# An attention and density kernel: bank-wise dependences for one-bank jobs, the last two density units in turn, and a later end for the density

## The chip, the cores and the metric

The kernel runs on one core of a Trainium2 chip. The metric is the device time of one execution in microseconds. The runs shown of the kernel before are 4967.25, 4970.23 and 4970.26 us, median 4970.23. A profile is one more execution, recorded by the hardware profiler.

In the text PE or TensorE is the matmul engine (PEld its weight loads), DVE or VectorE the vector engine, ACT or ScalarE the scalar engine, POOL or GpSimd the general engine, SP or SyncE the engine that issues most transfers.

## The reference, cut to what matters

The input is x, 8 images of 192 channels by 64 x 64 positions, all float32. Two layers follow one another, each with a residual addition.

```python
# layer 0: attention over the N = 4096 positions of an image, queries and keys of 24 channels
v = _gn(x)                                   # group norm, 32 groups
q = prelu(conv1x1(v, w1, b1), a1)            # [24, N]
k = prelu(conv1x1(v, w2, b2), a2)            # [24, N]
w = prelu(conv1x1(v, wa, ba), aa)            # [192, N]
score = softmax(q.T @ k, axis=2)
x = x + (score @ w.T).T
# layer 1: a density of every element, by a small network per channel (1-3-3-3-1)
y = _gn(x)
lower, upper = net(y - 0.5), net(y + 0.5)    # net: softplus(m) @ z + b, then z + tanh(f) * tanh(z)
s = -sign(lower + upper)
x = x + maximum(abs(sigmoid(s * upper) - sigmoid(s * lower)), 1e-6)
```

The group norm needs sums over a whole image, so the density of an image can start only when the attention of that image has ended; the queries, keys and values of an image need only the norm of the input.

## The kernel before, in words

The program is one long stream of attention steps, with all other work written between them by a planner that runs when the program is built. There is no loop on the chip: the order on each engine is the order in which the planner emits.

**The stream.** An image has 8 tiles of 512 queries (`NB`), and a tile has 16 steps (`STEPS`), each for 256 keys; so an image takes 128 steps (`IMG`) and the eight images 1024 (`last`). Step t does: the score products of step t+1 (`scores`, L738) into the PSUM tile `sc`; the products for the row maxima of a later tile (`max_step`, L669), 22 steps ahead (`LEAD`), into the PSUM tile `mx`, followed by their reduction on DVE (L677); the exponential on ACT (L742) from `sc` into `e`; and the products of `e` with the values (`attend`, L753). There is only one `mx` and one `sc` tile, each of two banks, so the products of a step wait until the reduction and the exponential of the step before have read them.

**Turns and jobs.** Two more PSUM tiles, `turns` (names `b0` and `b1`), of two banks each, take the attention sums of the tiles alternately. While one collects, the other serves as room for all other PSUM work: this is a *job*. `start_job` takes one job a step from a list ordered by rank, finds a room with enough free banks (`homes`, a tile and for each bank the step until which it is taken), hands the job a two-bank tile or one bank of it, and books its later parts with `at(step, function, costs)`. Jobs of one bank are:

- `norm_end`: the sums over a group by a product with `gavg` (mean L420, variance L433) and their readers on DVE (`second` L425, `third` L438), followed by `root` on ACT and `fourth` on DVE;
- `weights`: small products with the norm (L506, L511, L516), read by `offsets` on DVE (L525, L530);
- `keys`: the products for the keys (L573), read twice by ACT in `prelu` (L558), which DVE then combines (L561);
- `max_end`: the maxima of a tile are collected on DVE (L697, L700), transposed on PE (`turn`, L705) and added into the queries on DVE (`add`, L710).

Jobs of two banks are `queries` (L602), `values` (L630) and `finish` (the transposes L786 of a tile's outputs, and the residual addition L795 on DVE).

The dependences between instructions come from the tile framework. It knows a tile as a whole here: a write into one bank of `b0` waits for an earlier reader of the other bank of `b0` too.

**The head.** Before the stream the first image's queries, keys, values and the first maxima are made. There `homes` has four rooms at first: the two turns and two tiles `sc_head` and `mx_head` (`others`), which later carry the first maxima.

**The density.** An image's density is 12 units (`Unit`): two halves c, three channel thirds g, and s for lower and upper. A unit has 23 operations on DVE (`stt`, L995, all 128 x 1024) and its tanh and scaling operations on ACT (L963, L972, L978, L988). Up to three units are open at once (`units`, the oldest first). `density_step` runs at the end of each step: it gives each engine a credit and lets the open units emit while the credit is positive. For DVE the credit grows by `rate`, which is the time of the operations left of the oldest image divided by the steps left until step 10 of the image after next, and is capped at twice `rate`; other DVE work that the planner emits is taken from the credit. An operation on DVE that needs an ACT result needs it from an earlier step. When a pair s = 0, 1 of a third is done, `ending` forms the difference (POOL in the stream, DVE in the tail: `alone`, L1139 to L1149) and stores the result (L1161 and the transfers after it).

Units of image b are made when the second norm of image b is known, some 12 steps into the next image's attention. The density of the last image comes after the stream; there 11 of its 12 units do a part of their sums on PE (`product`, L936), in the PSUM tiles `b0`, `b1`, `sc_tail`, `mx_tail`. What is left of image 6 at step 1024 is emitted in the tail as well, in credits of `RATE` = 4.15 us a step.

**Loads.** The residual input `xc` of half an image has three buffers; a load is requested at steps 6 and 70 of an image and starts when a buffer is free, which is when the store of an earlier density's third g = 2 has been emitted. `finish` of a tile waits, in planner steps, until its half is loaded.

Of the kernel before, what the change touches and what calls it, by code (L numbers as in the profile page):

```python
# [17 lines left out]
def kernel(  # L18
# [306 lines left out]


    homes = []

    scratch = []
    for k, cols in (("a", F), ("b", 2 * C)):  # L330
# [3 lines left out]
            pair.append(u)  # L334
        scratch.append(pair)
    ready = [0, 0]

    def start_job(t):
        p = t % STEPS
        for n, (rank, make, hold, banks, cols) in enumerate(jobs):  # L340
            if stream[0] and (p < 3 or p + max(hold, 1) >= STEPS):
                continue
            rooms = [(pm, g) for pm, g in homes if sum(k <= t for k in g) >= banks]
            if not rooms:
                if rank < 2:
                    return
                continue
            k = [i for i in (1, 0) if ready[i] <= t and scratch[i][0].shape[1] >= cols]
            if cols and not k:
                continue  # L350
            del jobs[n]
            pm, guest = min(rooms, key=lambda r: max(r[1]))
            at_ = [i for i in range(2) if guest[i] <= t]
            for i in at_[:banks]:
                guest[i] = t + hold + 1
            if cols:
                ready[k[0]] = t + 2
            parts = make(pm if banks == 2 else pm[:, at_[0], :], scratch[k[0]] if cols else None)
            for i, fn, cost, act, pe in parts:
                at(t + i, fn, cost, act, pe)  # L360
            return
# [47 lines left out]
    def norm_end(key, n, t, then=None):  # L409
# [7 lines left out]

        def mean():
            pm = cell["pm"]
            nc.tensor.matmul(pm[:, 0:2], lhsT=gavg, rhs=cell["mv"], start=True, stop=True)  # L420

        def second():
            mv, pm = cell["mv"], cell["pm"]
            res = cell["res"] = small.tile([128, 2], F32, tag="nrm", bufs=4, name=f"nrm_{nm}")
            nc.vector.tensor_copy(res, pm[:, 0:2])  # L425
            dv = cell["dv"] = small.tile([128, 2], F32, tag="dv", name=f"dv_{nm}")
            nc.vector.tensor_tensor(dv[:, 0:1], mv[:, 0:1], res[:, 0:1], ALU.subtract)
            nc.vector.tensor_tensor(dv[:, 0:1], dv[:, 0:1], dv[:, 0:1], ALU.mult)
            nc.vector.tensor_copy(dv[:, 1:2], dv[:, 0:1])

        def variance():
            pm = cell["pm"]
            nc.tensor.matmul(pm[:, 2:4], lhsT=gavg, rhs=cell["dv"], start=True, stop=True)  # L433

        def third():
            res, pm = cell["res"], cell["pm"]
            ve = cell["ve"] = small.tile([128, 1], F32, tag="ve", name=f"ve_{nm}")
            nc.vector.tensor_tensor(ve, res[:, 1:2], pm[:, 2:3], ALU.add)  # L438
# [36 lines left out]

        def make(pm, _):
            cell["pm"] = pm
            return [
                (0, mean, 0.0, 0.0, 0.4), (1, second, 0.8, 0.0, 0.0),
                (2, variance, 0.0, 0.0, 0.4), (3, third, 0.4, 0.0, 0.0),  # L480
            ]
# [7 lines left out]
    def weights(b, then):  # L489
        res = norms[b, 0]  # L490
        cell = {}

        def scale():
            for k, src, n in (("q", w1r, 2), ("k", w2r, 1), ("v", wa_sb, 1)):
                d = wf[k, b] = fold.tile(
                    [128, 3, src.shape[2]], F32, tag=f"w{k}", bufs=n, name=f"w{k}_{b}"
                )
                nc.scalar.activation(d, src, AF.Copy, scale=res[:, 1:2])
            mb = cell["mb"] = fold.tile([128, 128], F32, tag="mb", name=f"mb_{b}")
            nc.vector.tensor_copy(mb, res[:, 0:1].to_broadcast([128, 128]))  # L500

        def products():
            pf = cell["pf"]
            p = slice(0, R)
            for g in range(3):
                nc.tensor.matmul(  # L506
                    pf[:, 0:2], lhsT=wf["q", b][p, g, :], rhs=res[p, 0:2],
                    start=g == 0, stop=g == 2,
                )
            for g in range(3):  # L510
                nc.tensor.matmul(  # L511
                    pf[:, 2:4], lhsT=wf["k", b][:, g, :], rhs=res[:, 0:2],
                    start=g == 0, stop=g == 2,
                )
            for g in range(3):
                nc.tensor.matmul(  # L516
                    pf[:, 4 : 4 + C], lhsT=cell["mb"][p], rhs=wf["v", b][p, g, :],
                    start=g == 0, stop=g == 2,
                )

        def offsets():
            pf = cell["pf"]
            for k, src, at_, n in (("bq", bq, 0, 2), ("bk", bk, 2, 1)):
                d = wf[k, b] = fold.tile([128, 2], F32, tag=k, bufs=n, name=f"{k}_{b}")
                nc.vector.tensor_tensor(  # L525
                    d[:, 0:1], src[:, 0:1], pf[:, at_ : at_ + 1], ALU.subtract
                )
                nc.vector.tensor_scalar(d[:, 1:2], d[:, 0:1], -1.0, None, ALU.mult)
            d = wf["ba", b] = fold.tile([128, C], F32, tag="ba", name=f"ba_{b}")
            nc.vector.tensor_tensor(d, ba_row, pf[:, 4 : 4 + C], ALU.subtract)  # L530
            then()

        at(now[0] + 1, scale, 0.3, 2.0)
        def make(pf, _):
            cell["pf"] = pf
            return [(0, products, 0.0, 0.0, 2.0), (1, offsets, 1.0, 0.0, 0.0)]

        at(now[0] + 3, lambda: job(make, 1))


# [8 lines left out]

    made = set()  # L550

    def prelu(name, dst, src, bias, nslope, u):


        def first():
            for i, sign in enumerate((1.0, -1.0)):
                b_ = bias[:, i : i + 1] if bias is not None else 0.0
                nc.scalar.activation(u[i], src, AF.Relu, bias=b_, scale=sign)  # L558

        def last():  # L560
            nc.vector.scalar_tensor_tensor(dst, u[1], nslope, u[0], ALU.mult, ALU.add)  # L561
            made.add(name)

        return first, last

    def keys(b, d, what, done):
        t = xi[what, b, d]

        def make(pk, u):
            if b not in kt:  # L570
                kt[b] = kpool.tile([128, N // 4], F32, tag="k", name=f"k_{b}")
            for g in range(3):
                nc.tensor.matmul(  # L573
                    pk[:, 0:P], lhsT=wf["k", b][:, g, :], rhs=t[:, g, :],
                    start=g == 0, stop=g == 2,
                )
# [4 lines left out]
            first, last = prelu(  # L581
                ("k", b, d), kt[b][p, at_ : at_ + P], pk[p, 0:P], wf["bk", b][p], nslope[p, 1:2],
                [x[p, 0:P] for x in u],
            )
            return [
                (0, lambda: None, 0.0, 0.0, 1.3), (1, first, 0.0, 0.9, 0.0),
# [104 lines left out]
    def max_end(b, n):  # L691
# [10 lines left out]
        def turn():  # L702
            pt = cell["pt"]
            for t in range(4):
                nc.tensor.transpose(pt[:, t * 128 : (t + 1) * 128], nm[:, t, :], ident)  # L705

        def add():
            u = (n % 2) * 256
            q = qt[b, n // 2][:, :, u : u + 256]
            nc.vector.tensor_tensor(  # L710
                q, q, cell["pt"].rearrange("p (s t) -> p s t", s=2), ALU.add
            )
            made.add(("max", b, n))

        def make(pt, _):
            cell["pt"] = pt
            return [(0, turn, 0.0, 0.0, 0.8), (1, add, 0.7, 0.0, 0.0)]

        at(now[0], collect, 0.4)
# [140 lines left out]
    class Unit:  # L860
# [146 lines left out]
        def more(self, k):  # L1007
# [6 lines left out]
            if (n, j) == (3, 2):  # L1014
                for q in range(3):
                    self.give(("l", 2, q))
                b, c, g, s = self.key
                if s == 1:
                    ending(b, c, g)

        def need(self):
# [244 lines left out]
    for d in range(NP):  # L1266
# [1 line left out]
            norm_stat((0, 0), 2 * d + k, flat(xi["first", 0, d], k))  # L1268
    spread()
    negatives()  # L1270
    others = [
        ps_sc.tile([128, 2, F], F32, tag="sc", name="sc_head"),
        ps_mx.tile([128, 2, F], F32, tag="mx", name="mx_head"),
    ]
    homes.extend((t, [0, 0]) for t in turns + others)

    def go_on():
# [103 lines left out]
```

## Time and profile before

| what | value |
|---|---|
| runs | 4967.25, 4970.23, 4970.26 us, median 4970.23 |
| the profiled execution's own time | 4970.59 us |
| its span, first to last instruction | 4968.6 us |
| granted TensorE clock, mean | 0.984 |
| busy in the span | PE 4785.8, DVE 4301.2, ACT 3202.4, POOL 513.9 us |
| first exponential of the stream | at 95.3 us |
| last exponential of the stream | at 4613.0 us |
| images 0 to 7 of the stream | 554.3, 569.9, 575.3, 572.8, 574.2, 572.8, 574.3, 524.1 us |
| after the stream | some 356 us |

The image times are read from the starts of the exponentials (L742): image b begins with the exponential of its step 0. The page sums busy time over the whole span; since the stages have different limits (the stream, the norm of the last image, its density), it is read together with tables of stretches. In lists of waits a line gives the waiting engine and instruction, what ended the wait, the total in us, the number of waits and the longest. A timeline's line gives start, duration, engine, line, operation, tiles and shapes, the number of instructions merged, and in brackets the idle time of the engine before it with what ended it.

### The profile page before, as it was taken

What the parts mean: (1) busy time and instruction counts of PE and PEld (TensorE: products, weight loads), DVE (VectorE), ACT (ScalarE), POOL (GpSimd) and SP (SyncE); (2) the same over time, 40 slices, a digit from 0 to 9 for tenths busy, and PEclk for the clock granted to TensorE, in tenths of its full rate; (3) what the DMA queues carried; (4) which work ended last, traced back from release to release, by engine and by line L of the source; (5) the groups of instructions that cost most, each with busy time, mean ns of one, the idle gap of its engine ahead of it and who ended that gap; (6) DMA issues with size and microseconds to landing.
All of it is one profiled execution on the core that took longest, in us unless ns stands there. A gap on an engine that the chain in (4) does not pass through costs nothing.

```text
span 4968.6 us, 69863 instructions
## 1 busy us (share of the span) xinstructions
PE 4785.8 (96%) x29152; PEld 3525.8 (71%) x29152; DVE 4301.2 (87%) x4442; ACT 3202.4 (64%) x3709; POOL 513.9 (10%) x506
## 2 busy tenths in 40 slices
PE   7999999999999999999999999999999999999596
PEld 5777777777777777777777777777777777777242
DVE  5433359999899989999899999999899999999888
ACT  2333346776667767777667766776677766776665
POOL 0000001111012110112011210110101110110000
PEclk9999999999999999999999999999999999999798
DMA  2000020011200111010200111011111111000000
GB/s 57 24 23 17 14 52 15 21 24 35 49 18 18 41 37 34 22 34 24 60 15 21 41 27 40 18 35 31 31 34 28 27 29 24 11 20 7 9 11 15
DMA packets 111953, 135.48 MB, mean 27 GB/s; under 512 B 14739, under 2 KB 93077, under 8 KB 111637
## 3 DMA queue, kind: packets, MB, share of 16 engines
q1 hardware_dynamic: 110432, 130.65, 10.9%
q8 instruction: 228, 3.74, 0.3%
q14 instruction: 89, 0.72, 0.1%
q10 hardware_dynamic: 1204, 0.37, 0.0%
HBM read 105.82 MB, written 25.17 MB: 26 GB/s over the span
## 4 chain that ended last, share of the span: by engine, by line
PE 73%; DVE 22%; ACT 3%; issue 1%; POOL 1%; DMA 0%; POOLq 0%; ACTq 0%; SPq 0%; DVEq 0%
PE b L753 43%; PE sc L738 17%; DVE d L995 14%; DVE rm L677 5%; PE b L630 3%; PE b L936 2%; PE b L602 1%; PE b L573 1%; PE mx L669 1%; PE sc_tail L936 1%; PE mx_tail L936 1%; PE b L786 1%; ACT d L988 1%; ACT d L963 1%; PE b L705 1%
## 5 line engine op out<-in xcount | busy, mean ns | idle before, releaser
L753 PEld LDWEIGHTS b<-v,e 128*128 128x128 f32 x16384 | 2668.4, 191 | 781.5 <-issue 781.5
L753 PE MATMUL b<-v,e 128*128 128x193 f32 x16384 | 2972.7, 335 | 0.0
L742 ACT ACTIVATE e<-sc 128x1024 f32<-128x1024 f32 x1024 | 1046.3, 1022 | 1422.6 <-PE mx L669 1373.3
L677 DVE TENSOR_REDUCE rm<-mx 128x1 f32<-128x1024 f32 x1002 | 1222.0, 1220 | 522.2 <-PE mx L669 518.5
L738 PE MATMUL sc<-q,k 25*128 25x512 f32 x4096 | 1159.7, 642 | 5.5 <-ACT e L742 5.2
L669 PE MATMUL mx<-k,q 24*128 24x512 f32 x4008 | 1135.6, 643 | 13.1 <-DVE rm L677 13.0
L995 DVE SCALAR_TENSOR_TENSOR d<-d,wsp,d 128x1024 f32<-128x1024 f32 x768 | 985.8, 1284 | 47.5 <-ACT d L988 35.4
L995 DVE SCALAR_TENSOR_TENSOR d<-d,lc,d 128x1024 f32<-128x1024 f32 x765 | 968.4, 1279 | 16.3 <-ACT d L972 3.3
L995 DVE SCALAR_TENSOR_TENSOR d<-d,tf,d 128x1024 f32<-128x1024 f32 x543 | 681.5, 1280 | 4.0 <-ACT d L978 3.9
L978 ACT ACTIVATE d<-d 128x1024 f32<-128x1024 f32 x543 | 570.1, 1055 | 70.8 <-DVE d L995 69.3
L738 PEld LDWEIGHTS sc<-q,k 25*128 25x128 f32 x4096 | 306.8, 183 | 238.6 <-issue 198.8
L1077 POOL MEMSET pause<- 128x1 f32 x240 | 23.7, 99 | 4007.4 <-DVE d L995 4007.4
L988 ACT ACTIVATE d<-d,cb,wsp 128x1024 f32<-128x1024 f32 x351 | 433.1, 1235 | 6.6 <-DVE d L995 5.3
L963 ACT ACTIVATE d<-xc,bn,wn 128x1024 f32<-128x1024 f32 x288 | 353.2, 1233 | 7.8 <-DVE bn L467 7.0
L669 PEld LDWEIGHTS mx<-k,q 24*128 24x128 f32 x4008 | 300.2, 183 | 40.1 <-DVE rm L677 39.9
L972 ACT ACTIVATE d<-xc,bn,wn 128x1024 f32<-128x1024 f32 x255 | 314.6, 1234 | 0.1
L1124 POOL TENSOR_TENSOR d<-d,d 128x512 f32<-128x512 f32 x80 | 167.9, 2098 | 0.1
L1112 POOL TENSOR_TENSOR d<-d,d 128x512 f32<-128x512 f32 x80 | 166.3, 2079 | 7.7 <-DVE d L995 7.1
L1132 POOL TENSOR_TENSOR d<-d,d 128x512 f32<-128x512 f32 x80 | 159.3, 1992 | 2.1 <-POOL pause L1077 0.3
L630 PE MATMUL b<-wv,xi 64*128 64x192 f32 x1344 | 139.5, 340 | 0.0
L630 PEld LDWEIGHTS b<-wv,xi 64*128 64x128 f32 x1344 | 106.5, 186 | 25.4 <-issue 23.8
L1116 ACT ACTIVATE d<-d 128x512 f32<-128x512 f32 x160 | 91.8, 623 | 32.1 <-POOL d L1112 26.0
(171 smaller groups left out, 2372.3 us busy)
## 6 DMA issues: line engine op xcount, KB each, us to landing
xi<-in_x_dram SPq DMA_DIRECT2D x392, 192.0 KB, 3.6
xc<-in_x_dram SPq DMA_DIRECT2D x64, 384.0 KB, 8.2
out_dram<-xc SPq DMA_DIRECT2D x96, 256.0 KB, 3.2
d<-in_x_dram SPq DMA_DIRECT2D x16, 192.0 KB, 4.3
d<-in_wat_dram ACTq DMA_DIRECT2D x2, 144.0 KB
cb<-in_den_b_dram SPq DMA_DIRECT2D x6, 2.2 KB, 2.1
ff<-in_den_f_dram SPq DMA_DIRECT2D x6, 2.2 KB, 2.1
bq<-in_b_dram ACTq DMA_DIRECT2D x4, 0.1 KB
```

Source lines behind the costliest of these rows:

```text
L630: nc.tensor.matmul(pv[:, s, 0:C], lhsT=t[p, g, k * 128 : k * 128 + 128] if g < 3 else one_row[p], rhs=wf["v", b][p, g, :] if g < 3 else wf ...
L669: nc.tensor.matmul(sc[:, s, :], lhsT=tile_of(qt[b, n // 2], n, j)[r], rhs=kt[b][r, u : u + F], start=True, stop=True,)
L677: nc.vector.tensor_reduce(out=rowmax[b, n][:, j, k : k + 1], in_=sc, axis=AX.XY, op=ALU.max)
L738: nc.tensor.matmul(sc[:, s, :], lhsT=kt[b][r, k : k + 128], rhs=qt[b, n // 2][r, :, u : u + 256], start=True, stop=True,)
L742: return lambda: nc.scalar.activation(e, sc, AF.Exp)
L753: nc.tensor.matmul(a[:, j, 0 : C + 1], lhsT=e[:, s, j * 128 : j * 128 + 128], rhs=v[:, s, p % 4, :], start=p == 0 and s == 0 and j % 2 == ...
L936: nc.tensor.matmul(out[:, h, :], lhsT=diag[g][:, 3 * i + n - 1 if n else 9 + i, :], rhs=src[:, h * F : h * F + F], start=n == 0, stop=n == 3,)
L963: nc.scalar.activation(self.buf[k], self.src(), AF.Tanh, bias=bn[:, s, g, 0, i : i + 1], scale=wn[:, g, 0, i : i + 1],)
L972: nc.scalar.activation(self.buf[k], self.src(), AF.Identity, bias=bn[:, s, g, 1, i : i + 1], scale=wn[:, g, 1, i : i + 1],)
L978: nc.scalar.activation(self.buf[k], self.buf["l", k[1], k[2]], AF.Tanh)
L988: nc.scalar.activation(self.buf[k], self.buf["l", n - 1, 0], AF.Identity, bias=offset, scale=wsp[:, g, w : w + 1],)
L995: nc.vector.scalar_tensor_tensor(dst, src, factor, dst, ALU.mult, ALU.add)
```

## The change

Three things are changed, and the order of the planner's decisions follows from them.

1. For one-bank jobs a matmul that writes bank i of a turn (or head tile) n is declared free of dependences on readers in the group `turn{n}{1-i}`, and each reader of bank i joins the group `turn{n}{i}`. It is done for `norm_end`, `weights`, `keys` and `max_end`; two-bank jobs are left as they were. The two head tiles are allocated earlier in the program, so that they have numbers.
2. When exactly two units are open, the one with more DVE operations left goes first, on each engine and in each step, and a unit is removed from the list when it has no DVE operation left, wherever it stands. The ending of a pair starts when both of its units are done, whichever is last.
3. `rate` counts the steps until step 15, not 10, of the image after next.

```diff
+    spot = [None]
+    def spotted():
+        n, i = spot[0]
+        def write(inst):
+            tc.declare_no_dep(inst.ins, group=f"turn{n}{1 - i}", reason="reads the other bank")
+        def read(inst):
+            tc.add_to_no_dep_group(f"turn{n}{i}", inst.ins)
+        return write, read
...
             if cols:
                 ready[k[0]] = t + 2
+            spot[0] = next(n for n, k in enumerate(turns + others) if k is pm), at_[0]
...
-            nc.tensor.matmul(pm[:, 2:4], lhsT=gavg, rhs=cell["dv"], start=True, stop=True)
+            cell["write"](
+                nc.tensor.matmul(pm[:, 2:4], lhsT=gavg, rhs=cell["dv"], start=True, stop=True)
+            )
...
-            nc.vector.tensor_tensor(ve, res[:, 1:2], pm[:, 2:3], ALU.add)
+            cell["read"](nc.vector.tensor_tensor(ve, res[:, 1:2], pm[:, 2:3], ALU.add))
...
+            write, read = spotted()
             for g in range(3):
-                nc.tensor.matmul(
+                write(nc.tensor.matmul(
                     pk[:, 0:P], lhsT=wf["k", b][:, g, :], rhs=t[:, g, :],
                     start=g == 0, stop=g == 2,
-                )
+                ))
...
                 b, c, g, s = self.key
-                if s == 1:
+                if not any(u.key == (b, c, g, 1 - s) and u.todo["DVE"] for u in units):
                     ending(b, c, g)
...
-            rate = left * COST["DVE"] / max(1, (units[0].key[0] + 2) * IMG + 10 - t) + OTHER
+            rate = left * COST["DVE"] / max(1, (units[0].key[0] + 2) * IMG + 15 - t) + OTHER
...
-            for n in range(min(3, len(units))):
+            order = list(range(min(3, len(units))))
+            if len(units) == 2:
+                order.sort(key=lambda n: -len(units[n].todo["DVE"]))
+            for n in order:
                 units[n].step(eng, t, list(units)[:n])
-        while units and not units[0].todo["DVE"]:
-            units.popleft()
+        for u in [u for u in units if not u.todo["DVE"]]:
+            units.remove(u)
```

The same wrapping by `write` and `read` is made in `weights` (`products`, `offsets`), in `max_end` (`turn`, `add`), in `norm_end`'s other two places and around the two ACT readers of the keys in `prelu`.

More of the change, by code (lines that the diff above doesn't have):

```diff
@@ L327 @@
     homes = []
+    others = [
+        ps_sc.tile([128, 2, F], F32, tag="sc", name="sc_head"),
+        ps_mx.tile([128, 2, F], F32, tag="mx", name="mx_head"),
+    ]
     scratch = []
@@ L419, in mean @@
             pm = cell["pm"]
-            nc.tensor.matmul(pm[:, 0:2], lhsT=gavg, rhs=cell["mv"], start=True, stop=True)
+            cell["write"](
+                nc.tensor.matmul(pm[:, 0:2], lhsT=gavg, rhs=cell["mv"], start=True, stop=True)
+            )
         def second():
@@ L424, in second @@
             res = cell["res"] = small.tile([128, 2], F32, tag="nrm", bufs=4, name=f"nrm_{nm}")
-            nc.vector.tensor_copy(res, pm[:, 0:2])
+            cell["read"](nc.vector.tensor_copy(res, pm[:, 0:2]))
             dv = cell["dv"] = small.tile([128, 2], F32, tag="dv", name=f"dv_{nm}")
@@ L432, in variance @@
             pm = cell["pm"]
-            nc.tensor.matmul(pm[:, 2:4], lhsT=gavg, rhs=cell["dv"], start=True, stop=True)
+            cell["write"](
+                nc.tensor.matmul(pm[:, 2:4], lhsT=gavg, rhs=cell["dv"], start=True, stop=True)
+            )
         def third():
@@ L477, in make @@
             cell["pm"] = pm
+            cell["write"], cell["read"] = spotted()
             return [
@@ L505, in products @@
             for g in range(3):
-                nc.tensor.matmul(
+                cell["write"](nc.tensor.matmul(
                     pf[:, 0:2], lhsT=wf["q", b][p, g, :], rhs=res[p, 0:2],
                     start=g == 0, stop=g == 2,
-                )
+                ))
             for g in range(3):
-                nc.tensor.matmul(
+                cell["write"](nc.tensor.matmul(
                     pf[:, 2:4], lhsT=wf["k", b][:, g, :], rhs=res[:, 0:2],
                     start=g == 0, stop=g == 2,
-                )
+                ))
             for g in range(3):
-                nc.tensor.matmul(
+                cell["write"](nc.tensor.matmul(
                     pf[:, 4 : 4 + C], lhsT=cell["mb"][p], rhs=wf["v", b][p, g, :],
                     start=g == 0, stop=g == 2,
-                )
+                ))
         def offsets():
@@ L524, in offsets @@
                 d = wf[k, b] = fold.tile([128, 2], F32, tag=k, bufs=n, name=f"{k}_{b}")
-                nc.vector.tensor_tensor(
+                cell["read"](nc.vector.tensor_tensor(
                     d[:, 0:1], src[:, 0:1], pf[:, at_ : at_ + 1], ALU.subtract
-                )
+                ))
                 nc.vector.tensor_scalar(d[:, 1:2], d[:, 0:1], -1.0, None, ALU.mult)
             d = wf["ba", b] = fold.tile([128, C], F32, tag="ba", name=f"ba_{b}")
-            nc.vector.tensor_tensor(d, ba_row, pf[:, 4 : 4 + C], ALU.subtract)
+            cell["read"](nc.vector.tensor_tensor(d, ba_row, pf[:, 4 : 4 + C], ALU.subtract))
             then()
@@ L535, in make @@
             cell["pf"] = pf
+            cell["write"], cell["read"] = spotted()
             return [(0, products, 0.0, 0.0, 2.0), (1, offsets, 1.0, 0.0, 0.0)]
@@ L550, with prelu @@
     made = set()
-    def prelu(name, dst, src, bias, nslope, u):
+    def prelu(name, dst, src, bias, nslope, u, read=lambda inst: None):
         def first():
@@ L557, in first @@
                 b_ = bias[:, i : i + 1] if bias is not None else 0.0
-                nc.scalar.activation(u[i], src, AF.Relu, bias=b_, scale=sign)
+                read(nc.scalar.activation(u[i], src, AF.Relu, bias=b_, scale=sign))
         def last():
@@ L571, in make @@
                 kt[b] = kpool.tile([128, N // 4], F32, tag="k", name=f"k_{b}")
+            write, read = spotted()
             for g in range(3):
-                nc.tensor.matmul(
+                write(nc.tensor.matmul(
                     pk[:, 0:P], lhsT=wf["k", b][:, g, :], rhs=t[:, g, :],
                     start=g == 0, stop=g == 2,
-                )
+                ))
             done()
@@ L582, in make @@
                 ("k", b, d), kt[b][p, at_ : at_ + P], pk[p, 0:P], wf["bk", b][p], nslope[p, 1:2],
-                [x[p, 0:P] for x in u],
+                [x[p, 0:P] for x in u], read,
             )
@@ L704, in turn @@
             for t in range(4):
-                nc.tensor.transpose(pt[:, t * 128 : (t + 1) * 128], nm[:, t, :], ident)
+                cell["write"](
+                    nc.tensor.transpose(pt[:, t * 128 : (t + 1) * 128], nm[:, t, :], ident)
+                )
         def add():
@@ L709, in add @@
             q = qt[b, n // 2][:, :, u : u + 256]
-            nc.vector.tensor_tensor(
+            cell["read"](nc.vector.tensor_tensor(
                 q, q, cell["pt"].rearrange("p (s t) -> p s t", s=2), ALU.add
-            )
+            ))
             made.add(("max", b, n))
@@ L716, in make @@
             cell["pt"] = pt
+            cell["write"], cell["read"] = spotted()
             return [(0, turn, 0.0, 0.0, 0.8), (1, add, 0.7, 0.0, 0.0)]
@@ L1270 @@
     negatives()
[L1271 to L1274, printed above, removed]
     homes.extend((t, [0, 0]) for t in turns + others)
```

## The prediction

> **What bounds the kernel now.** I read the page's busy shares first, then a table by stretches cut at image boundaries, then the waits of the matmul engine, then timelines.
>
> ```profile
> PE 4785.8 (96%) x29152; PEld 3525.8 (71%) x29152; DVE 4301.2 (87%) x4442; ACT 3202.4 (64%) x3709; POOL 513.9 (10%) x506
> ```
>
> TensorE is nearly always busy, but the page warns that matmul ends are modelled. The stretches (width, then busy time of PE, PEld, DVE, ACT, POOL) separate the limits: image 0, a middle image, image 7, the norm chain after the last attention step, the last density, the end.
>
> ```profile
> 95.30:649.60 554.30, 553.24 (x3553) 419.46 (x3554) 206.44 (x287) 171.78 (x227) 0.00 (x0) 1.00 0.07 19
> ...
> 2367.60:2941.80 574.20, 567.54 (x3579) 427.85 (x3579) 546.81 (x557) 403.63 (x468) 76.70 (x72) 0.99 0.13 31
> ...
> 4088.90:4613.00 524.10, 521.77 (x3117) 389.12 (x3117) 489.14 (x467) 370.50 (x401) 61.67 (x60) 1.00 0.07 15
> 4613.00:4661.00 48.00, 9.83 (x44) 8.01 (x45) 43.88 (x65) 30.39 (x57) 0.00 (x0) 0.58 0.04 11
> 4661.00:4940.00 279.00, 235.41 (x527) 101.10 (x525) 235.90 (x194) 186.09 (x175) 0.00 (x0) 0.95 0.05 12
> 4940.00:4968.60 28.60, 0.00 (x0) 0.00 (x0) 16.11 (x13) 9.68 (x9) 0.00 (x0) 0.50 0.07 18
> ```
>
> Image 0 has nearly the same matmuls as a middle image (3553 against 3579) and no density. It takes 554.3 us with VectorE busy for 206: that is TensorE's own pace. A middle image takes 574.2, so some 20 us are stalls, while VectorE is busy for 547. Both engines are close to full, and each waits for the other in turn. The recorded waits of TensorE in images 1 to 7:
>
> ```profile
> PE mx L669 <- DVE rm L677: 13.0, 18, 1.5
> PE b L573 <- DVE q L710: 12.0, 12, 2.7
> PE b L705 <- DVE ve L438: 11.6, 5, 2.3
> PE sc L738 <- ACT e L742: 3.0, 9, 1.0
> PE b L705 <- ACT prb L558: 2.1, 5, 0.4
> ```
>
> Lines two and three are waits for a reader of the other bank: the keys (L573) for the add of the maxima (L710), the transposes of the maxima (L705) for the norm's variance (L438). All four are one-bank jobs. Line five is a reader of two banks (`prb`, the values) and stays. Line one is true: the next score product needs the running maximum read out. A stretch of image 4 shows how these waits meet:
>
> ```profile
> 2412.49 2.88 PE L753 MATMUL b<-v,e 128*128 128x193 f32 x16
> ...
> 2415.90 1.22 DVE L677 TENSOR_REDUCE rm<-mx 128x1 f32<-128x1024 f32 x1
> ...
> 2417.69 0.66 PE L705 MATMUL b<-ident,negmax 128*128 128x128 f32 x4 [2.33 <-DVE ve L438]
> ...
> 2419.49 4.38 PE L753 MATMUL b<-v,e 128*128 128x193 f32 x16
> ...
> 2443.74 6.29 DVE L995 SCALAR_TENSOR_TENSOR d<-d,lc,d 128x1024 f32<-128x1024 f32 x5
> ...
> 2451.22 1.13 PE L669 MATMUL mx<-k,q 24*128 24x512 f32 x4 [1.51 <-DVE rm L677]
> ```
>
> The wait of 2.33 us is followed by an attention step of 4.38 instead of 2.88. At 2443.74 the new image's density begins with five operations at once, since density had nothing to do in the two steps before and its credit stood at the cap; the reduce behind them comes late. In 2403 to 2451 (steps 8 to 17 of the image) VectorE is busy for 39.4 of 48 us: both engines have room there.
>
> **Part 1, the banks.** No instruction is added; waits go. L573: 12 waits, 12.0 us (8.0 of it in images 2 to 6, so 1.6 an image; 4.0 in image 1). Behind the keys nothing else is late: after the wait at 2568.74 it is VectorE that idles for 2.78 us. So I count them whole. L705: of 2.33 us only some 1.1 can be won, for the reduce at 2415.90, queued on VectorE behind density, ends at 2417.12, and the products of the next step wait for that: they start at 2418.28 now, at about 2417.2 then. Five of these make 5.5.
>
> Then the clock. The trace has 4.38 - 2.88 = 1.5 us lost in the attention step after each of the five L705 waits, and about as much after the longest L573 wait (2.7 us, image 1): 6 x 1.5 = 9. [...] by the trace 26.5. I take the trace: gaps of 2.3 us were followed by the slow step. Of the 26.5, the L573 share is 12.0 + 1.5 = 13.5; the L705 share of 13 lies in just the steps that part 3 fills, and is reckoned there. In the head keys also run in one bank, but TensorE is busy without a gap from 32 us until its scores at 93: between 0 and -2 us, I take 0.
>
> **Part 3, density up to step 15.** An image's density is 12 units of 23 operations on L995, 276. Its start is step 12 of the next image; the planner spreads it to step 138 now, 143 then: 276/126 = 2.19 a step against 276/131 = 2.11. At step 138 some 5 x 2.1 = 10.5 operations are then still to do. At 6.29/5 = 1.26 us each that is 13 us of VectorE moved from steps 13 to 138 into steps 10 to 15, in images 2 to 7, and from image 7 into the tail.
>
> Receiving end: 39.4 + 13.2 us, less about three of the burst of five, which the older units push back (3.8): 48.8, with gaps some 49.5 where 48 passes now. So the region becomes VectorE's, and costs +1.5 us although its stalls (2.4 and 1.5 at L705, 2.6 and 1.7 at the burst) vanish. This is where part 1's L705 share goes.
>
> Giving end: steps 17 to 137 lose 9 us of VectorE work. It helps only where TensorE is late because of VectorE. Comparing each block of score products and attention steps of image 4 with its usual length, I find 6.8 us of such lateness there (around 2485, 2500, 2580 to 2592, 2765); half of it, -3.5. In the rest VectorE merely idles more.
>
> Images 2 to 6: 1.5 - 3.5 - 1.6 = -3.6, times 5 = -18. Image 1 (no older density arrives): -4.0 - 1.5 - 2 = -7.5. Image 7: lateness 13 us, a third of it, -4, and +1.5: -2.5.
>
> What else moves: an image's last store comes some four steps later (step 24 instead of 20), so the load of the residual input (SyncE's queue, issued at steps 21 and 22 now) and the first tile's transposes (step 25 now) slip to steps 28 to 30. Three steps of room remain before that tile's outputs would be overwritten. Cover: the tile waits in SBUF. Without it the next evacuation would stall: -0 to +2 us an image; I take 0.
>
> **Part 2, the last two units in turn.** In the stream VectorE has no unit-latency gaps to fill (its waits there are for L669), so 0, between -1 and +1 an image through fewer bursts. In the tail:
>
> ```profile
> 4643.71 2.60 DVE L995 SCALAR_TENSOR_TENSOR d<-d,wsp,d 128x1024 f32<-128x1024 f32 x2 [1.54 <-ACT d L988]
> ...
> 4648.57 2.60 DVE L995 SCALAR_TENSOR_TENSOR d<-d,wsp,d 128x1024 f32<-128x1024 f32 x2 [1.61 <-ACT d L988]
> ...
> 4942.17 2.60 DVE L995 SCALAR_TENSOR_TENSOR d<-d,wsp,d 128x1024 f32<-128x1024 f32 x2 [2.25 <-ACT d L988]
> ...
> 4947.09 2.61 DVE L995 SCALAR_TENSOR_TENSOR d<-d,wsp,d 128x1024 f32<-128x1024 f32 x2 [2.31 <-ACT d L988]
> ```
>
> A lone last unit waits for ScalarE between its pairs. In turn, the partner fills 2.25 + 2.31 = 4.6 us at the end (I take 4) and 3.1 us in 4613 to 4661. That stretch receives 13 us from image 7 and had 4.1 idle: 13 - 3.1 = +10; as the last of it may run on beside the density of image 7, where VectorE idles for 43 of 279 us, +8. Tail: +8 - 4 = +4. Moving the two head tiles' allocation issues nothing: 0.
>
> **Sum.** -18 - 7.5 - 2.5 + 4 = -24. Against the profiled execution's own 4970.6 us (span 4968.6; the median of the runs, 4970.2, is the same within 0.4) that is 4946.
>
> **Rivals.**
> 1. The two engines interlock so well after it that lateness goes whole (6.8 an image, 13 in image 7) and the region stays at 48 us. Images 2 to 6: -8.4 x 5 = -42; image 1: -9.5; image 7: -8; tail +4: 4915. For it: VectorE idles for 27 us in image 4. Against: TensorE's own 554 us, and the many steps where TensorE is not late, in which an idle VectorE gains nothing.
> 2. VectorE's overload in steps 8 to 17 wins (slower). If none of the new image's operations give way, it needs 39.4 + 13.2 + 1 = 53.6 us there: +5.6 in each of images 2 to 7, +33.6; nothing gained from lateness; tail +10; L573 -13.5: 5001. It decides from about 51 us in that region. For it: the norm chain, statistics and tile endings all lie there, and TensorE has one buffer of maxima. Against: older units go first and share one credit.
> 3. The bank edit has no effect, another wait on the same engine standing behind each removed one: the 13.5 of L573 are missing, 4960.
>
> **How the numbers follow.** Forecast 0.50 (own range 4928 to 4962), rival 1 0.20, rival 2 0.17, rival 3 0.13. This kernel can be told from no change at about 0.2%, 10 us. Faster: nearly all of the forecast, rival 1, half of rival 3: 0.72. Within: 0.13. Slower: most of rival 2: 0.15. The range 4910 to 4976 leaves out about 0.08 below and 0.12 above.
>
> **What would show it.** Right: L573 <- L710 and L705 <- L438 gone from the waits; no 4.38 us step behind L705; no burst of five at step 16; images 2 to 6 at 568 to 571 us, image 1 at 562; the stretch from the last attention step to the last density's first PE sum at some 56 us; the last two waits for L988 gone. Wrong: middle images unchanged or over 576, or L669 <- L677 grown by more than the 20 us that left the other lines.

## The result, and the profile after

The changed kernel takes 4934.16 us in the median of four runs (4930.91 to 4944.02), the kernel before 4970.24 of four; the ratio is 0.993, interval 0.9913 to 0.9948. The forecast was 4946, faster. The profiled execution took 4931.85 us with a span of 4929.8, 38.8 less than before.

The total hides two opposite parts. First the stretches of the kernel after, cut at the same places as those of before (width, then busy PE, PEld, DVE, ACT, POOL, the granted clock, the DMA share and GB/s): images 1, 4 and 7, the norm after the stream, the last density, the end.

```profile
650.00:1210.90 560.90, 559.92 (x3579) 424.77 (x3579) 513.03 (x527) 381.72 (x443) 55.58 (x53) 0.99 0.12 30
...
2344.50:2911.00 566.50, 562.52 (x3579) 424.37 (x3580) 547.12 (x557) 403.27 (x467) 76.38 (x73) 1.00 0.13 31
...
4044.20:4561.20 517.00, 515.72 (x3117) 386.36 (x3117) 493.62 (x468) 370.66 (x402) 75.78 (x69) 1.00 0.07 16
4561.20:4620.00 58.80, 9.47 (x44) 8.05 (x45) 56.68 (x74) 40.34 (x66) 0.00 (x0) 0.58 0.04 9
4620.00:4900.00 280.00, 236.09 (x527) 101.26 (x525) 232.95 (x194) 186.85 (x177) 0.00 (x0) 0.94 0.05 12
4900.00:4929.80 29.80, 0.00 (x0) 0.00 (x0) 19.39 (x16) 9.47 (x9) 0.00 (x0) 0.50 0.07 18
```

Image 4 went from 574.2 to 566.5 us with the same 547 us of VectorE work, and its mean clock from 0.99 to 1.00. All eight images together won 52 us (they took 4517.7 and 4465.5). The tail lost 12.9: from the start of the last exponential to the end it takes 368.5 us, 355.6 before, and nearly all of that is in the first stretch, 58.8 against 48.0, of which VectorE is now busy for 56.7.

Second, the waits of TensorE from image 1 to the end of the stream:

```profile
PE mx L697 <- DVE rm L705: 14.6, 18, 1.5
PE sc L769 <- ACT e L773: 7.3, 12, 1.1
```

These are all that are left. L697 is the old L669, L705 the old L677. The waits of the keys and of the transposes for readers of the other bank (12.0 and 11.6 us) are gone, and so is the wait for `prb` (2.1) that the edit does not touch: in the new order it no longer comes about. Part of what was removed came up elsewhere: the true wait for the maxima grew from 13.0 to 14.6 us and the wait for the exponentials (L769, the old L738) from 3.0 to 7.3, together 5.9 of the 23.6.

The trace also records when TensorE's clock was granted at half. Before, this was so for 58.0 us in 15 spells between 600 us and the end of the stream; after, for 6.8 us in two spells, both in image 1. By an estimate from these figures, half of the 51 us between them, that is worth at most some 25 us, about half of what the stream won.

### The profile page after: what moved, and what is told of

The parts are those of the page before. It is cut to its first block, busy times and chain, and to the rows that moved or that the text cites. A ratio compares the mean times of both kernels' runs of the same rounds, so it can differ in the third digit from the quotient of the medians.

```text
span 4929.8 us, 69894 instructions
## 1 busy us (share of the span) xinstructions
PE 4754.2 (96%) x29152; PEld 3507.0 (71%) x29152; DVE 4310.0 (87%) x4442; ACT 3201.4 (65%) x3709; POOL 516.3 (10%) x506
## 4 chain that ended last, share of the span: by engine, by line
PE 81%; DVE 14%; ACT 3%; issue 1%; POOL 1%; DMA 0%; SPq 0%; ACTq 0%; POOLq 0%; DVEq 0%
PE b L784 49%; PE sc L769 18%; DVE d L1026 9%; PE b L658 4%; DVE rm L705 3%; PE b L967 2%; PE b L630 2%; PE b L601 2%; PE mx L697 1%; PE sc_tail L967 1%; PE mx_tail L967 1%; PE b L817 1%; ACT d L1009 1%; ACT d L1019 1%; DVE st L427 0%
## 5 line engine op out<-in xcount | busy, mean ns | idle before, releaser
L705 DVE TENSOR_REDUCE rm<-mx 128x1 f32<-128x1024 f32 x1002 | 1223.2, 1221 | 477.4 <-PE mx L697 472.6
L769 PE MATMUL sc<-q,k 25*128 25x512 f32 x4096 | 1154.9, 640 | 9.6 <-ACT e L773 9.6
L697 PE MATMUL mx<-k,q 24*128 24x512 f32 x4008 | 1130.2, 640 | 14.6 <-DVE rm L705 14.6
L1026 DVE SCALAR_TENSOR_TENSOR d<-d,lc,d 128x1024 f32<-128x1024 f32 x765 | 981.0, 1291 | 19.6 <-ACT d L1003 5.1
L769 PEld LDWEIGHTS sc<-q,k 25*128 25x128 f32 x4096 | 306.2, 183 | 241.9 <-issue 196.2
L1019 ACT ACTIVATE d<-d,cb,wsp 128x1024 f32<-128x1024 f32 x351 | 433.7, 1235 | 2.9 <-DVE d L1026 2.2
L697 PEld LDWEIGHTS mx<-k,q 24*128 24x128 f32 x4008 | 299.6, 183 | 39.7 <-DVE rm L705 35.2
L967 PE MATMUL b<-d,v 128*128 128x512 f32 x204 | 94.6, 615 | 17.3 <-ACT d L994 17.3
```

Of the source, the lines that this page charges most:

```text
L697: nc.tensor.matmul(sc[:, s, :], lhsT=tile_of(qt[b, n // 2], n, j)[r], rhs=kt[b][r, u : u + F], start=True, stop=True,)
L705: nc.vector.tensor_reduce(out=rowmax[b, n][:, j, k : k + 1], in_=sc, axis=AX.XY, op=ALU.max)
L769: nc.tensor.matmul(sc[:, s, :], lhsT=kt[b][r, k : k + 128], rhs=qt[b, n // 2][r, :, u : u + 256], start=True, stop=True,)
L967: nc.tensor.matmul(out[:, h, :], lhsT=diag[g][:, 3 * i + n - 1 if n else 9 + i, :], rhs=src[:, h * F : h * F + F], start=n == 0, stop=n == 3,)
L1019: nc.scalar.activation(self.buf[k], self.buf["l", n - 1, 0], AF.Identity, bias=offset, scale=wsp[:, g, w : w + 1],)
L1026: nc.vector.scalar_tensor_tensor(dst, src, factor, dst, ALU.mult, ALU.add)
```

## The experiments

The three parts are called banks (1), turns (2) and step 15 (3). Each kernel is the one after with parts undone, or with a small addition. "Middle images" is the mean of images 2 to 6, "half clock" the time at half clock between 600 us and the end of the stream; both are of the profiled execution. The time is the median of the runs, with the ratio to the kernel before on the same chip. Differences between two changed kernels are those of these medians; taken against each one's own kernel before they shift by up to 2 us.

| kernel | time, us | ratio and interval | middle images | image 7 | tail | half clock |
|---|---|---|---|---|---|---|
| before | 4966.8 to 4970.4 | 1 | 573.9 | 524.1 | 355.6 | 58.0 |
| banks | 4948.95 | 0.9961 (0.9948 to 0.9974) | 570.2 | 524.1 | 356.3 | 27.3 |
| turns | 4948.01 | 0.9964 (0.9951 to 0.9977) | 570.0 | 523.6 | 356.0 | 44.4 |
| step 15 | 4995.93 | 1.0056 (1.0041 to 1.0071) | 577.7 | 530.8 | 361.4 | 75.1 |
| banks, turns | 4921.63 | 0.9903 (0.9886 to 0.9919) | 565.2 | 523.7 | 355.8 | 30.7 |
| banks, step 15 | 4992.23 | 1.0050 (1.0033 to 1.0066) | 577.4 | 530.8 | 361.3 | 85.3 |
| turns, step 15 | 4959.73 | 0.9987 (0.9980 to 0.9994) | 571.0 | 517.2 | 369.4 | 30.7 |
| all three (after) | 4934.16 | 0.9930 (0.9913 to 0.9948) | 566.7 | 517.1 | 368.5 | 6.8 |

### One part alone, or one part undone

**Banks alone.** The unit order and the step of before are put back:

```diff
-            if len(units) == 2:
+            if False:
...
-            rate = left * COST["DVE"] / max(1, (units[0].key[0] + 2) * IMG + 15 - t) + OTHER
+            rate = left * COST["DVE"] / max(1, (units[0].key[0] + 2) * IMG + 10 - t) + OTHER
```

> The bank edit alone: one-bank jobs free of readers of the other bank, density to step 10, no turns, so the order on every engine is that of before. Prediction's sum by itself: 12.0 us of L573 waits, 5.5 of L705 waits, 9 of slow clock, -26 us to about 4944, and image 1 about -5. Rival (the freed engine meets the next wait at once, the late reduce): only the 13.5 of L573, about 4957. Clock theory: the gain is mostly half-clock time: of the 15 half-clock spells between 600 and 4500 us the five behind L705 and the one at 849 go, 9 stay (those behind the burst of five at step 16), and a middle image comes to 568 to 570 us.

Measured: -19.3 us, between the sum (-26) and the rival (-13.5). Half-clock spells fell from 15 to 7, a middle image to 570.2. So the edit acts, and by more than the bare L573 waits: the interval of the ratio reaches down to -12.9 us, about the rival's figure, but eight clock spells are gone, and the rival counts one. A third of the 23.6 us of bank waits was lost again: the waits for the maxima rose from 13.0 to 14.6 us, those for the exponentials from 3.0 to 9.1.

**Step 15 alone.** Banks and turns undone: `spotted` returns functions that do nothing, and the unit order is that of before.

> The density up to step 15 alone, bank waits and unit order as before. Prediction's sum: lateness -3.5 and region +1.5 in five images, image 1 -2, image 7 -2.5, tail +8: about 4964. Rival (the burst of five at step 16 goes and its 4.3 us with it, nothing is lost in steps 8 to 17): -4 to -8 an image, tail +10, about 4940 to 4950. Overlap theory (banks and step 15 remove the same stalls): as large in the stream as the bank edit alone, middle image 568 to 570. The L573 and L705 waits stay in the list in any case.

Measured: +27.7 us, on the other side of every figure expected. A middle image takes 577.7, image 7 6.7 us longer, and half-clock time rises to 75.1. The waits of TensorE for the maxima rose from 13.0 to 36.7 us. The bank waits were expected to stay and did not: in the new order those of the keys fell from 12.0 to 6.1 us, and those of the transposes for the variance are gone, with the bank edit undone.

**All but banks.**

> The whole change without the bank edit. If the bank edit carries the clock gain: the spells behind L705 come back, a middle image 571 or more, total 4955 to 4962. If order and deadline carry it: middle image at most 568, total about 4940.

Measured: 4959.73, a middle image 571.0, the figures of the first case, but not by its way: no spell stands behind the transposes (one wait of 0.8 us is left there). In images 2 to 6 all spells but one stand behind waits of 1.46 us for the maxima, at a place where the kernel after has the same waits and no spell. The banks are worth 26 us on top of the other two, as much on top of the turns, 19 alone, but only 4 on top of step 15.

**All but turns.**

```diff
-            if len(units) == 2:
+            if False:
```

> The whole change without the last two units in turn. Prediction: the turns are worth 4 us at the end and 3 us in the tail's first stretch, so 4941. Rival (the last unit's own chain sets the end whatever the partner does): the end stays as it is, 4934 within 3. If the turns matter in the stream by smoothing: middle image above 568.

Measured: 4992.23. Neither the 4941 of the prediction nor the 4934 of the rival: without the turns the change is slower than before. The end of the tail, from the last matmul on, is 36.4 us with turns and 35.2 without: the turns win nothing where I had looked for it. They win it in the stream, as the third case had it (a middle image above 568).

### Why step 15 loses without the turns

The trace of "all but turns", VectorE and TensorE around the end of one image's density and the start of the next (start, duration, what; in brackets the idle time and its cause):

```profile
2430.97 2.60 DVE L1026 SCALAR_TENSOR_TENSOR d<-d,wsp,d 128x1024 f32<-128x1024 f32 x2
...
2433.48 2.48 DVE L1026 SCALAR_TENSOR_TENSOR d<-d,tf,d 128x1024 f32<-128x1024 f32 x2
...
2435.87 1.28 DVE L1026 SCALAR_TENSOR_TENSOR d<-d,lc,d 128x1024 f32<-128x1024 f32 x1
...
2437.07 1.22 DVE L705 TENSOR_REDUCE rm<-mx 128x1 f32<-128x1024 f32 x1
...
2438.34 1.54 PE L697 MATMUL mx<-k,q 24*128 24x512 f32 x4 [1.11 <-DVE rm L705]
...
2438.75 5.09 DVE L1026 SCALAR_TENSOR_TENSOR d<-d,lc,d 128x1024 f32<-128x1024 f32 x4
...
2439.82 4.10 PE L784 MATMUL b<-v,e 128*128 128x193 f32 x16
...
2443.76 1.22 DVE L705 TENSOR_REDUCE rm<-mx 128x1 f32<-128x1024 f32 x1
...
2445.82 1.27 DVE L1026 SCALAR_TENSOR_TENSOR d<-d,tf,d 128x1024 f32<-128x1024 f32 x1
...
2447.01 2.60 DVE L1026 SCALAR_TENSOR_TENSOR d<-d,wsp,d 128x1024 f32<-128x1024 f32 x2
...
2449.52 2.60 DVE L1026 SCALAR_TENSOR_TENSOR d<-d,lc,d 128x1024 f32<-128x1024 f32 x2
...
2452.04 1.22 DVE L705 TENSOR_REDUCE rm<-mx 128x1 f32<-128x1024 f32 x1
...
2453.31 2.08 PE L697 MATMUL mx<-k,q 24*128 24x512 f32 x4 [3.28 <-DVE rm L705]
```

Five, four and again five density operations stand between one reduce (L705) and the next in three steps. The reason is read from the planner's code. A lone unit may use on VectorE only what ScalarE was given in an earlier step (none to two operations between two reduces in the ten before these), so it cannot spend its credit. `rate` is work left divided by steps left, so it rises as the deadline nears, and the credit may hold two rates. When the new image's units open, all of it is spent at once, the reduce of the maxima comes late, TensorE waits up to 3.3 us, and slow attention steps follow (4.10 us at 2439.82, behind a wait of 1.11, instead of the 2.88 of a step in time). In the kernel after, the same stretch shows at most three operations between two reduces:

```profile
2409.54 1.22 DVE L705 TENSOR_REDUCE rm<-mx 128x1 f32<-128x1024 f32 x1
2410.67 0.55 DVE L427 BATCH_NORM_STATS2 st<-xi 128x6 f32<-128x384 f32 x1
2411.14 0.74 DVE L588 SCALAR_TENSOR_TENSOR q<-pra,nslope,pra 128x512 f32<-128x512 f32 x1
2411.79 1.28 DVE L1026 SCALAR_TENSOR_TENSOR d<-d,wsp,d 128x1024 f32<-128x1024 f32 x1
2412.99 1.28 DVE L1026 SCALAR_TENSOR_TENSOR d<-d,tf,d 128x1024 f32<-128x1024 f32 x1
2414.18 1.28 DVE L1026 SCALAR_TENSOR_TENSOR d<-d,wsp,d 128x1024 f32<-128x1024 f32 x1
2415.38 1.22 DVE L705 TENSOR_REDUCE rm<-mx 128x1 f32<-128x1024 f32 x1
```

To test this I kept the turns out and forbade the bursts:

```diff
+                if eng == "DVE":
+                    if t < last and count[0] >= 3:
+                        return
+                    count[0] += 1
                 todo.popleft()
```

> Banks and step 15 without the turns, and a cap: at most three density operations on VectorE in a step of the stream. Burst theory (a lone last unit cannot use its credit, the rate rises as its deadline nears, and bursts of four and five operations put the reduce late): most of the loss goes, middle image 565 to 571 instead of 577, half-clock time in the stream under 40 us instead of 85, total 4940 to 4955. Rival (the lone unit's work simply ends too late and lies in the wrong steps): middle image above 574, total above 4975.

Measured: 4946.30 (0.9961, 0.9949 to 0.9974), middle images 569.9, half clock 23.9 us instead of 85.3. The waits of TensorE for the maxima fell from 39.8 us in all to 7.6. The cap alone returns 46 of the 58 us that the missing turns cost. So the bursts were most of the loss; the rival, that the lone unit's work merely comes too late, is refuted. The other 12 us are not explained.

**The turns alone.**

> The last two units in turn alone: bank waits as before, density to step 10. If the turns smooth VectorE's load by themselves: middle image 568 to 571, total 4940 to 4955. If they only pay together with the bank edit (the bursts they avoid met the same waits): total within 5 us of before. The prediction's own figure for the stream was 0.

Measured: 4948.01, -18.8. The turns need neither of the other parts. In the trace the waits for the maxima fell from 13.0 to 7.8 us; those for a reader of the other bank rose from 23.6 to 36.3, which fits that the banks are worth more once the turns are there. Alone, banks and turns give -19.3 and -18.8; together -47.1, so they help each other by 9 more.

The lists of waits show only a part of what a late reduce costs. This is TensorE in the kernel with banks and turns, a step in time and a late one:

```profile
2418.22 0.70 PE L769 MATMUL sc<-q,k 25*128 25x512 f32 x2
2418.23 0.70 PE L697 MATMUL mx<-k,q 24*128 24x512 f32 x2
...
2419.28 2.88 PE L784 MATMUL b<-v,e 128*128 128x193 f32 x16
2422.10 1.13 PE L769 MATMUL sc<-q,k 25*128 25x512 f32 x4
2424.21 1.13 PE L697 MATMUL mx<-k,q 24*128 24x512 f32 x4 [0.99 <-DVE rm L705]
2425.27 2.88 PE L784 MATMUL b<-v,e 128*128 128x193 f32 x16
```

In time, the products for the scores and for the maxima overlap and take 1.06 us together, from 2418.22 to 2419.28. Late, they run one after the other and take 3.17 with the wait: 2.1 us lost, of which the list shows 0.99. In images 2 to 6 this happens in 25 steps before and in 15 with the turns alone. With the banks it is not rarer (31 alone, 33 with the turns, 30 in the kernel after), so there the gain lies in the waits and the clock.

### What step 15 is worth once the turns are there

**Banks and turns, step 10.**

> Banks and turns, density to step 10 as before. If the later end is what the turns make possible (the gain of the step needs the turns, but the turns alone give little): as the bank edit alone, 4946 to 4950, tail first stretch about 46 us, middle image 569 to 571. If the turns are the gain and the step is not: about 4934 or less, since the tail keeps 46 us instead of 57.

Measured: 4921.63 (four runs, 4919.2 to 4922.3). This version beats both kernels: -47 us against before, and its runs all lie below those of the kernel after, though the two intervals against before overlap a little. The later end is not the gain. It costs 12.7 us of tail, wins 6.6 in image 7 and 3.7 in image 1, and loses 1.5 in each middle image.

**The last image spread to step 10, then to step 5**, the others to step 15. In the first, 15 in `rate` becomes

```diff
-(units[0].key[0] + 2) * IMG + 15 - t
+(units[0].key[0] + 2) * IMG + (15 if units[0].key[0] < B - 2 else 10) - t
```

> The whole change, but image 6's density, the one that runs into the tail, is spread to step 10 only; the other images to 15. Theory (density left for the tail is paid there in full, about 1.2 us an operation, and image 7 has 23 us of idle VectorE): 27 operations instead of 37 in the tail, first stretch 46 to 48 us instead of 57, image 7 at 517 to 521: total 4923 to 4929. Rival (image 7 is at the limit of both engines, so it pays what the tail saves): image 7 at 528, total 4934.

> The same with image 6's density to step 5: some 17 operations in the tail. Theory: first stretch 33 to 38 us, image 7 with 25 us more VectorE work than after against 23 idle: 524 to 530; total 4918 to 4926. Rival (image 7 pays): 4934 or more; a further rival: the first stretch is set by the chain of the norm and does not fall below 42, total 4928 to 4936.

Measured: 4934.00 and 4942.97. At step 10 the tail came down from 368.5 to 360.0, as expected, and image 7 rose from 517.1 to 525.2: image 7 paid what the tail saved, as the rival had it. At step 5 the tail is 351.7, image 7 537.2; the tail's stretch up to the density's first products takes 40.4, less than the 42 of the further rival and more than the theory's 33 to 38. VectorE's 23 us of idle time in image 7 were no room: with 502.1 and 516.6 us of work instead of 493.6 it is still idle for 23.1 and 20.6.

**Banks and turns at step 12.**

> Banks and turns with the density to step 12, between the 10 of before and the 15 of the change. If the later end costs in proportion (each step moves some two operations from image 7 to the tail, where they are paid in full): tail 360 to 362 us, total 4925 to 4930. If the gain of an image lies in filling steps 11 to 15 and is only hidden by the tail: middle image below 563 and total below 4921. If the middle image is set by where the bursts happen to fall: 562 to 572, in no order with the step.

Measured: 4948.77 (0.9956, 0.9939 to 0.9973), 27 us slower than at step 10 and 15 slower than at 15, so not in proportion. The middle images show it, 565.2, 569.8 and 566.7 at steps 10, 12 and 15. Both kernels have a burst of five at the start of a density, 6.3 us long; the late step shown above stands behind that of step 10. This is TensorE at step 12, around the same place:

```profile
2415.24 0.98 PE L769 MATMUL sc<-q,k 25*128 25x512 f32 x2 [2.29 <-ACT e L773]
...
2417.03 3.80 PE L784 MATMUL b<-v,e 128*128 128x193 f32 x16
...
2435.05 1.17 PE L697 MATMUL mx<-k,q 24*128 24x512 f32 x4 [1.51 <-DVE rm L705]
2436.15 4.47 PE L784 MATMUL b<-v,e 128*128 128x193 f32 x16
```

At step 10 the burst falls behind a reduce alone; at step 12 statistics and a reciprocal stand in the same step, the wait is half a microsecond longer (1.51 against 0.99), and a slow step follows. The longer wait is the first one, for an exponential: three activations of the new density, 1.2 us each, stand ahead of it on ScalarE. It comes in each of images 2 to 6, and the waits for exponentials sum to 18.9 us at step 12 and 2.4 at step 10. In the stream, half-clock time is 54.6 us at step 12 and 30.7 at step 10.

**The cap of three on banks and turns, step 10.**

> Banks and turns, step 10, and the same cap of three. If the two bursts still there (four at step 9, five at step 15 of a middle image) cost what such bursts cost before: middle image 559 to 562 instead of 564, total 4895 to 4912. If the cap only moves the work: 4918 to 4925. If operations are left over and reach the tail: more than 4930.

Measured: 4928.31 (0.9921, 0.9906 to 0.9936), 7 us slower than without the cap; middle images 566.5. All the figures expected are missed: there is no further gain, the time lies above the 4918 to 4925 of mere moving, and nothing is left over for the tail, which takes 355.6 us as against 355.8. Here, where the burst of five costs a wait of 0.99 us and no slow step, forbidding it won nothing.

### The clock by itself

**Work in the wait.** The order and waits of before; ahead of the waiting transposes of images 2 to 6 stand three products that may run while they wait:

```diff
+            if n == 1 and 2 <= b <= 6:
+                for _ in range(3):
+                    cell["fill"](
+                        nc.tensor.matmul(
+                            pt[:, 0:384], lhsT=ident, rhs=w1r.rearrange("p g n -> p (g n)"),
+                            start=True, stop=True,
+                        )
+                    )
```

> The kernel before in its order and with its waits, only that in images 2 to 6 three products of 384 columns, free of the other bank's readers, stand ahead of the transposes that wait for the norm's variance: TensorE works through the wait of 2.3 us, and the wait itself stays. Clock theory: the five half-clock spells behind these waits go (15 to 10), 1.5 to 1.7 us each, image -1.5, total -7 to -8, about 4961. Rival (the wait is the whole cost, the slow steps after it have another cause): spells stay at 15, total unchanged or up to +3 where the products run longer than the wait.

TensorE in image 4 of this kernel:

```profile
2411.15 2.10 PE L735 MATMUL b<-w1r,ident 128*128 128x384 f32 x6
2413.64 0.66 PE L742 MATMUL b<-ident,negmax 128*128 128x128 f32 x4 [0.39 <-DVE ve L462]
2414.22 0.70 PE L777 MATMUL sc<-q,k 25*128 25x512 f32 x2
...
2415.29 2.88 PE L792 MATMUL b<-v,e 128*128 128x193 f32 x16
```

The transposes still wait for the variance, only 0.39 us of it idle, and the attention step behind takes 2.88 us where before had 4.38. (The view counts each of the three products as two.) Before has a spell behind these waits in images 3 to 6, this kernel in none. So the slow step came from TensorE's idleness, not from the wait's other effects. In all, half clock fell from 58.0 to 37.5 us and the time by 4.7 us (ratio 0.9993, 0.9984 to 1.0002): in the direction expected, short of the 7 to 8, and not clear of no change. Part of the 1.5 us came back as a new wait (TensorE now waits 1.0 us for an exponential at 2428).

**The same instructions in two phases.** The kernel with image 6's density spread to step 5 emits the same order on TensorE, VectorE and ScalarE as the kernel after until some 70 us into image 7. Its middle images took 569.6 us, those of after 566.7. This is one and the same place, the kernel after first:

```profile
2826.42 1.13 PE L697 MATMUL mx<-k,q 24*128 24x512 f32 x4 [1.46 <-DVE rm L705]
2827.48 2.88 PE L784 MATMUL b<-v,e 128*128 128x193 f32 x16
```

```profile
2832.55 2.08 PE L697 MATMUL mx<-k,q 24*128 24x512 f32 x4 [1.46 <-DVE rm L705]
2834.56 5.19 PE L784 MATMUL b<-v,e 128*128 128x193 f32 x16
```

The waits are equal, 1.46 us. One is followed by full clock, the other by 3.3 us of loss (2.31 in the attention step, 0.95 in the products); the clock record has half clock from 2832.4 to 2839.2 in the second and none here in the first. In the traces of before and after, the 17 spells between 600 us and the end of the stream last 3.41 or 6.83 us each, and in each trace they begin on one grid of 3.413 us, whose place differs between the two. The grid of after has a point at 2826.00 and splits the wait of the first into 1.03 and 0.42 us; of the second, some 1.3 us lie ahead of the start of its spell at 2832.4. Cut at their grids, from 600 us to the end of the stream, the two traces have 11 stretches at full clock with 1.3 us or more of TensorE's idle time, and half clock followed 10 of them; it followed none of the 4 with 1.0 to 1.3. These are counts and no rule: the other 7 spells begin behind stretches with less than 1.0 us, 5 of them with none, and what set those off is open. The kernel after has a spread between runs, 4930.9 to 4944.0, with mean clocks from 0.988 to 0.985; that the phase is its cause was not shown.

## Why the prediction was right, and where it was not

The total came within 12 us and the sign was right. That it came so near is in part luck: the images won 52 us where 28 were forecast, the tail lost 12.9 where 4 were. Of its terms, the first holds in the main, and two fail in opposite directions.

- **The bank waits** (12.0 and 5.5 us): right that they go, too high as a gain counted whole. L697 and the waits for exponentials grew by 5.9 us in the kernel after and by 7.7 with the banks alone. Rival 3, no effect at all, falls by the run with the banks alone.
- **The clock of part 1** (six spells of 1.5): right that spells go with the waits, the size was too small. Alone, the banks took 8 of 15 spells away, and the whole change 13. The prediction read from the trace that gaps of 2.3 us are followed by a slow step, and the runs show spells behind waits of 1.46, 1.51 and 2.33 us. It missed that a wait just as long can be free, so that a fixed 1.5 us a wait is a mean at best. The trace of before had shown it: the prediction reads a slow step after each of the five L705 waits, but in image 2 none follows:

```profile
1269.66 0.66 PE L705 MATMUL b<-ident,negmax 128*128 128x128 f32 x4 [2.33 <-DVE ve L438]
...
1271.32 2.88 PE L753 MATMUL b<-v,e 128*128 128x193 f32 x16
```

- **"In the stream VectorE has no unit-latency gaps to fill", 0 for part 2**: the step that failed. It looked for gaps on VectorE in the trace. What the turns change is not a gap but what the planner can spend: a lone unit leaves credit, and the credit becomes bursts. They are worth 18.8 us alone and 58 beside banks and step 15. That bursts are the way is shown by the cap beside banks and step 15; for the turns alone it is argued from the fewer late steps. At the end of the tail, where I gave them 4 us, they win none: one wait of 2.32 us for L1019 remains there, and the stretch after the last matmul is 1.2 us longer. Of the 3.1 us in the tail's first stretch they win 1.1 (46.2 and 45.1 us, before and turns alone).
- **Part 3, "-3.5 elsewhere, +1.5 in the region"**: fails in sign. Alone step 15 costs 27.7 us, on top of the other two 12.5 (10.1 in the two profiled executions). The argument by mean rates (2.19 operations a step against 2.11) left out the planner's capped credit, from which the bursts come.
- **The region around the start of a density**, forecast to become VectorE's and to cost 1.5 us. It did become VectorE's: from the exponential of step 8 to that of step 20 it is busy for 51.07 of 51.83 us. But this stretch got only 3.3 us of work more, not 9.4, and it is 5.2 us shorter instead of 1.5 longer; of that, 4.3 us lie in its last step, behind the burst of before. Which of the new image's operations gave way is not shown. The rest of the image won 2.5, where 5.1 was forecast. The stretch in image 4, first before, then after:

```profile
2401.03:2458.01 56.98, 53.14 (x309) 39.91 (x308) 47.73 (x65) 37.71 (x45) 11.18 (x12) 0.94 0.09 24
```

```profile
2377.69:2429.52 51.83, 50.99 (x309) 38.07 (x310) 51.07 (x68) 41.02 (x46) 4.55 (x6) 1.00 0.10 27
```

- **Image 1** (-7.5): measured -9.1. **Images 2 to 6** (-18): -36.1. **Image 7** (-2.5): -7.0. **Tail** (+4): +12.9, of it +11.2 up to the density's first products (+8 forecast; 46.2 to 57.4 us) and +1.7 later (-4 forecast).
- **Smaller slips**: rival 1 has image 7's lateness of 13 us go whole and yet counts -8 there; by its words it comes to 4910. In the head TensorE is not quite without a gap: it waits 1.1 us at 72.

Rival 2, the overload of steps 8 to 17, is what step 15 does without the turns, by bursts rather than by the sum of the work. Rival 1 came near in the stream (52 us of its 60) and is cut by the tail.

What stays open: why the middle images of step 10 beat those of step 15 by 1.5 us, though they have more half-clock time (30.7 us in the stream against 6.8). The two have different orders throughout, and no run separates order and clock phase.

## What to carry to other kernels

Where two engines are both nearly full, look at what stands between two instructions that the other engine needs, not at mean rates: four or five operations ahead of a needed reduce can cost more than the same work in portions of two or three (46 us in one kernel here, nothing in another). Undo each part of a compound change on the chip; here one of three parts was a loss that the other two outweighed. And with a scheduler of credits, ask what it does with credit that it can't spend.

## What was not expected of the hardware

A wait of 1.46 us on TensorE cost nothing in one execution and 3.3 us of slow clock in another, with the same instructions before it. In four of the five middle images such a spell came behind this wait, and four more came at other places; together they moved the five images by 14.8 us (2833.3 and 2848.1).
